# Loads and stores of a chunked product stage, in pieces of 64 KB

## The chip, the cores and the metric

The kernel runs on one core of one Trainium2 chip. The metric is the device time of one execution in microseconds (us), the median over runs. One further execution was recorded by the hardware profiler, and all views of the profile come from it.

## The reference

The input x has 16 samples of 128 x 1024 float32 values. Two blocks follow one another, each with a mixer and a feed-forward part, both added to x. The first block's feed-forward part is the one that matters here. It is a spectral filter, run along the 1024 positions of a sample, each with 128 channels:

```
Vf = rfft(phi, n); Uf_p = rfft(u, n); Uf_m = rfft(u * sign, n)
U_plus  = irfft(Vf[.., k, .] * Uf_p);  U_minus = sign * irfft(Vf[.., k, .] * Uf_m)
out = sum over k, d of (U_plus s_k M_plus[k, d, e] + U_minus s_k M_minus[k, d, e]) + short taps
```

Four such filters are mixed by weights. The mixing over 16 filters k and over the channels d and e is linear, so it can be done at each frequency: a matrix per frequency, made of the filters' spectra and the matrices M, multiplied with the spectra of all 16 samples. Attention, convolutions and a routed mixture of experts make up the rest.

## The kernel before

The kernel has three stretches. **Up to about 383 us** an attention stage and the forward transform run through the samples. For each sample, POOL writes the spectrum into a tile xf, and SP stores it into a DRAM tensor vd of shape [16 chunks, 128, 16 samples, 128 values] (line 627; for the last sample in two DMAs, chunk 0 first). SP also stores the sample's running sum x to a DRAM tensor xd (line 646), and loads mi, x and weights.

**From about 383 to 661 us** runs the product stage, the one that is changed. It loops over 16 chunks c of frequencies, and in each over four steps m.

- `begin(c)` (called with c + 1 in step m = 0 of chunk c) loads the chunk's spectra from vd, in four DMAs of four samples each into four tiles xc with one buffer per tile (line 793, 128 rows of 2 KB, 256 KB each), and POOL makes the tile v from each: two additions or subtractions (L796) and one negation (L797).
- `generate` computes, on PE, the matrices of the next chunk into PSUM tiles pg (L805; 64 matmuls as the profile counts them per step), and `collect` copies them to the tile g on DVE (L816) and ACT (L818).
- `multiply` multiplies v with g on PE into a PSUM tile py (L829; 64 per step). ACT copies py to yt (L891), and `combine` adds and subtracts the halves into a tile ys on DVE (L858, L859).
- `finish(c)`, after the last combine of a chunk, does four more operations on POOL (L843 to L846; on DVE for the last chunk) and stores ys into a DRAM tensor yd, in two DMAs of 128 rows of 4 KB (line 850, 512 KB each). The last two chunks go to a tensor of their own, yd[1].

v and ys have two buffers each, and the PSUM pool eight, shared by pg and py. In chunk 15 nothing is generated any more, so its four steps are products alone.

The order on PE, DVE, ACT and POOL is the order of the program text in this stage. The order on SP, which issues all these DMAs, is left to a planner that works from its own estimates. In its order SP issues three xc loads of chunk 0, then the last sample's two vd stores and its xd store, then nine xc loads (the fourth of chunk 0, those of chunks 1 and 2), and from there on two yd stores of chunk c and four xc loads of chunk c + 3 in turn. Behind the stores of chunk 13 stand loads for the next stretch (gw, gb, tmat, wi), then the stores of chunks 14 and 15. The DMAs that SP issues signal on eight semaphores in turn, so each also waits until the one eight before it has landed.

**From about 661 us** the inverse transform, convolutions, routing and experts run. Their first work waits for a load y from yd.

Of the kernel before, what the change touches and what calls it, by code (L numbers as in the profile page):

```python
# [14 lines left out]
P = 128  # L15
B, C, H, W = 16, 128, 32, 32
# [16 lines left out]
NCH = 16  # L33
# [7 lines left out]
RG = P // KR  # L41
# [28 lines left out]
def metaformer_kernel(ctx: ExitStack, tc: tile.TileContext, io: dict, out: bass.AP):  # L70
    nc = tc.nc
# [104 lines left out]
    with ExitStack() as l0:  # L176
# [3 lines left out]
        vd = dram.tile([NCH, P, B, CW], F32, name="vd", tag="vd")  # L180

        yd = [dram.tile([n, 2, B, 2 * NM, C], F32, name=f"yd{i}", tag=f"yd{i}")
              for i, n in enumerate((P - 2 * JL, 2 * JL))]
# [36 lines left out]
        with ExitStack() as a0:  # L220
# [537 lines left out]
            with tc.manual_schedule(engines=PINNED):  # L758
                for p in range(-reach, B):
                    next(preparing, None)  # L760
                    for name, d in period:
                        b = p + d
# [13 lines left out]
        with ExitStack() as g0:  # L776
# [8 lines left out]
            def begin(c):  # L785

                v = cpl.tile([P, 2 * NM * JL, 3, B], F32, name="v", tag="v")
                vs[c] = v
                vv = v.rearrange("p (x w) k b -> p x k b w", x=2)
                for i in range(B // BP):  # L790
                    bs = slice(i * BP, (i + 1) * BP)
                    xc = xcl.tile([P, BP, 2, 2, NM * JL], F32, name="xc", tag=f"xc{i}")
                    nc.sync.dma_start(xc.rearrange("p b x r w -> p b (x r w)"), vd[c, :, bs, :])
                    e, o = (xc[:, :, x].rearrange("p b r w -> p r b w") for x in range(2))
                    for x, op in enumerate((ALU.add, ALU.subtract)):
                        nc.gpsimd.tensor_tensor(vv[:, x, 1:, bs], e, o, op)  # L796
                    nc.gpsimd.tensor_scalar(v[:, :, 0, bs], v[:, :, 2, bs], -1.0, None, ALU.mult)  # L797
# [40 lines left out]
            def finish(c, ys):  # L838

                eng = nc.gpsimd if c + 1 < NCH else nc.vector  # L840
                e = cpl.tile([P, JL // RG, 2, C], F32, name="ye", tag="ye", bufs=1)
                yv = ys[:, :, 0]
                eng.tensor_tensor(e, yv[:, :, :2], yv[:, :, 2:], ALU.add)  # L843
                eng.tensor_tensor(yv[:, :, 2:], yv[:, :, :2], yv[:, :, 2:], ALU.subtract)
                eng.tensor_tensor(yv[:, :, 0], e[:, :, 0], e[:, :, 1], ALU.add)
                eng.tensor_tensor(yv[:, :, 1], e[:, :, 0], e[:, :, 1], ALU.subtract)  # L846
                for kl in range(JL // RG):
                    last = c + 2 >= NCH
                    j0 = kl * RG + (c - NCH + 2 if last else c) * JL
                    nc.sync.dma_start(  # L850
                        yd[last][j0 : j0 + RG].rearrange("g r b x e -> (g r b) (x e)"),
                        ys[:, kl].rearrange("p x m e -> p (x m e)"),
                    )

            def combine(c, m, ys, t):

                a, b = t
                nc.vector.tensor_tensor(ys[:, :, 0, m], b, a, ALU.add)  # L858
                nc.vector.scalar_tensor_tensor(ys[:, :, 1, m], b, -1.0, a, ALU.mult, ALU.add)  # L859
                if m == NM - 1:  # L860
                    finish(c, ys)

            with tc.manual_schedule(engines=PINNED):
                begin(0)
                gs[0] = gpl[0].tile([P, CW, C], F32, name="g", tag="g")
                for q in range(NB):
                    collect(0, q, generate(0, q))
                waiting = None
                for c in range(NCH):
                    if c + 1 < NCH:  # L870
                        gs[c + 1] = gpl[(c + 1) % 2].tile([P, CW, C], F32, name="g", tag="g")

                    ys = cpl.tile([P, JL // RG, 2, NM, C], F32, name="ys", tag="ys")
                    for m in range(NM):
                        if c + 1 < NCH:
                            pg = [generate(c + 1, 2 * m + x) for x in range(2)]
                            collect(c + 1, 2 * m, pg[0])
                        if waiting:
                            combine(*waiting)
                        if c + 1 < NCH:  # L880
                            if m == 0:
                                begin(c + 1)
                            collect(c + 1, 2 * m + 1, pg[1])
                        py = psg.tile([P, 2, JL // RG, C], F32, name="py", tag="p")
                        fresh = set()
                        for x in range(2):
                            multiply(c, m, x, py, fresh)
                        if c + 1 < NCH or m == 0:
                            t = cpl.tile([P, 2, JL // RG, C], F32, name="yt", tag="yt", bufs=1)
                        if c + 1 < NCH:  # L890
                            nc.scalar.copy(t, py)  # L891
                            waiting = c, m, ys, (t[:, 0], t[:, 1])
                        else:
                            nc.scalar.copy(t[:, m % 2], py[:, 0])
                            waiting = c, m, ys, (t[:, m % 2], py[:, 1])
# [14 lines left out]
    with ExitStack() as c1:  # L910
# [695 lines left out]
        with tc.manual_schedule(engines=PINNED):  # L1606
            yt = first.tile([P, 2, N], F32, name="yt", tag="v")
            for pr in (0, 1, 2, 3, 7, 4, 5, 6):
                py = [ps.tile([P, N], F32, name=f"pfy{j}", tag="pfy") for j in range(2)]
                for hf in range(2):  # L1610
                    cs = slice(hf * HALF, (hf + 1) * HALF)
                    for j in range(2):
                        js = slice(j * E, (j + 1) * E)
# [3 lines left out]
                for j in range(2):  # L1617
                    b = 2 * pr + j
# [162 lines left out]
```

## Time and profile before

| what | value |
|---|---|
| median of 3 runs (lowest, highest) | 1250.93 us (1250.57 to 1251.35) |
| profiled execution: time, span | 1249.26 us, 1247.5 us |
| busy, share of the span | PE 93%, PE weight load 76%, DVE 75%, ACT 58%, POOL 48% |
| product stage, 399 to 646 us (247.00 us): busy | PE 238.59, DVE 181.89, ACT 184.66, POOL 200.77 us |
| the same window: share of the DMA engines, rate | 0.39, 123 GB/s |
| loads xc<-vd | 64 DMAs of 256 KB, median 3.4 us to landing |
| stores yd<-ys | 32 DMAs of 512 KB, median 3.6 us to landing |
| DMA queue q1 (hardware, from SP) | 90448 packets, 170.46 MB |
| DMA queue q8 (instructions) | 113 packets, 1.85 MB |

The profiled execution has 1.76 us around its span, and lies 1.67 us under the median of the runs. A line such as "L829" is a line of the kernel before. PEld is the weight load that precedes a matmul and overlaps the one before it. SPq stands for SP's queue, where a row's duration is the time that the issue takes, not the transfer. In a row of groups or of the timeline, the bracket at the end gives the idle time of the engine before the work and what ended it. The granted clock of PE was 0.994 on average.

### The profile page before, as it was taken

The numbers are of one execution on the slowest core, as the hardware profiler recorded it, in microseconds if no ns is written. First come the engines' busy times: TensorE is split into PE (matmuls) and PEld (weight loads), VectorE is DVE, ScalarE is ACT, GpSimd is POOL, SyncE is SP. The second block draws the span as 40 slices with busy tenths as digits, with TensorE's granted clock in tenths as the row PEclk, the third lists the DMA queues.
The fourth block names the chain that finished last, engine by engine and source line by source line (L and its number), as shares of the span: only waits on it lengthen the run. The fifth ranks groups of instructions, "written<-read, shape, count | busy, mean of one in ns | idle before, by whom it ended". The sixth has DMA issues, their size and how long they took to land.

```text
span 1247.5 us, 34359 instructions
## 1 busy us (share of the span) xinstructions
PE 1166.0 (93%) x14398; PEld 952.3 (76%) x14398; DVE 940.9 (75%) x1944; ACT 725.2 (58%) x1420; POOL 603.1 (48%) x800
## 2 busy tenths in 40 slices
PE   7889999999999999999988899999999999998996
PEld 6667777776768898888887788888888888875443
DVE  5888888888766777777765689898898989884235
ACT  4777777877556777777751346555555556534111
POOL 2435545665568688888882434343333334220003
PEclk9999999999999999999999999999999999999998
DMA  7005344352436334444348422233332331416996
GB/s 279 24 31 168 118 135 132 117 173 90 137 119 211 105 115 138 139 129 127 128 128 277 121 51 54 84 101 118 115 106 85 102 102 51 152 43 240 384 406 279
DMA packets 91244, 175.14 MB, mean 140 GB/s; under 512 B 5969, under 2 KB 42065, under 8 KB 90449
## 3 DMA queue, kind: packets, MB, share of 16 engines
q1 hardware_dynamic: 90448, 170.46, 41.2%
q0 software_dynamic: 640, 2.49, 0.6%
q8 instruction: 113, 1.85, 0.6%
q14 instruction: 43, 0.34, 0.1%
HBM read 110.28 MB, written 62.65 MB: 139 GB/s over the span
## 4 chain that ended last, share of the span: by engine, by line
PE 60%; DVE 23%; ACT 7%; DMA 4%; issue 4%; POOL 2%; SPq 0%; POOLq 0%; ACTq 0%; DVEq 0%
PE pg L805 10%; PE pcv L988 10%; PE py L829 10%; PE big L638 6%; DVE bst L135 4%; PE big L152 3%; PE big L171 3%; PE big L570 2%; PE big L450 2%; PE big L533 2%; PE big L432 2%; DMA y<-yd 2%; DVE abss L1231 1%; DVE xp L1253 1%; ACT tt L144 1%
## 5 line engine op out<-in xcount | busy, mean ns | idle before, releaser
L988 PE MATMUL pcv<-v,cw 128*128 128x256 f32 x1152 | 259.9, 382 | 2.7 <-POOL v L1178 2.7
L988 PEld LDWEIGHTS pcv<-v,cw 128*128 128x128 f32 x1152 | 215.9, 191 | 36.3 <-issue 4.9
L818 ACT COPY g<-pg 128x512 f32<-128x512 f32 x316 | 161.1, 605 | 46.0 <-PE pg L805 45.3
L816 DVE COPY g<-pg 128x512 f32<-128x512 f32 x196 | 127.6, 682 | 69.4 <-PE pg L805 69.4
L805 PE MATMUL pg<-ph,mst 32*128 32x128 f32 x4096 | 144.2, 280 | 9.2 <-issue 8.2
L805 PEld LDWEIGHTS pg<-ph,mst 32*128 32x128 f32 x4096 | 128.7, 186 | 25.7 <-issue 16.7
L829 PE MATMUL py<-g,v 128*32 128x128 f32 x4096 | 125.1, 274 | 4.6 <-issue 2.3
L829 PEld LDWEIGHTS py<-g,v 128*32 128x32 f32 x4096 | 108.2, 110 | 12.7 <-POOL v L797 2.6
L144 ACT ACTIVATE tok<-tok,sts 128x128 f32<-128x128 f32 x256 | 101.9, 481 | 16.9 <-DVE sts L1065 13.6
L135 DVE BATCH_NORM_STATS2 bst<-big 128x6 f32<-128x256 f32 x256 | 91.1, 416 | 21.0 <-PE big L152 11.7
L796 POOL TENSOR_TENSOR v<-xc 128x256 f32<-128x256 f32 x128 | 99.0, 797 | 3.3 <-PE pg L805 2.3
L638 PE MATMUL big<-u,mu 128*128 128x128 f32 (+4 forms) x384 | 86.0, 380 | 0.0
L1178 POOL TENSOR_TENSOR v<-abss 128x256 f32<-128x256 f32 x64 | 49.1, 787 | 68.1 <-DVE abss L1174 56.7
L286 POOL TENSOR_TENSOR xf<-ab 128x256 f32<-128x256 f32 x34 | 24.8, 729 | 110.4 <-DVE ab L253 110.3
L1197 POOL TENSOR_TENSOR yo<-abss 128x256 f32<-128x256 f32 x32 | 23.5, 735 | 110.2 <-DVE abss L1193 110.2
L638 PEld LDWEIGHTS big<-u,mu 128*128 128x128 f32 x384 | 56.7, 191 | 18.0 <-issue 15.4
L570 PE MATMUL big<-wf,ub 128*128 128x256 f32 x256 | 62.0, 385 | 0.2
L144 ACT ACTIVATE tt<-tt,sts 128x128 f32<-128x128 f32 x128 | 51.1, 481 | 14.5 <-DVE sts L1065 14.5
L797 POOL TENSOR_SCALAR v<-v 128x256 f32<-128x256 f32 x64 | 55.7, 871 | 5.6
L475 POOL TENSOR_TENSOR ke<-ke,ks 128x1024 f32<-128x1024 f32 x16 | 30.6, 1914 | 54.8 <-DVE qs L483 43.8
L1622 POOL TENSOR_TENSOR xb<-yt,xb 128x1024 f32<-128x1024 f32 x3 | 7.1, 2355 | 96.9 <-ACT yt L1621 96.9
L570 PEld LDWEIGHTS big<-wf,ub 128*128 128x128 f32 x256 | 46.2, 190 | 8.8 <-ACT xn L423 3.0
(256 smaller groups left out, 2526.0 us busy)
## 6 DMA issues: line engine op xcount, KB each, us to landing
we<-in_weight SPq DMA_DIRECT2D x32, 1024.0 KB, 8.9
xc<-vd SPq DMA_DIRECT2D x64, 256.0 KB, 3.4
yd<-ys SPq DMA_DIRECT2D x32, 512.0 KB, 3.6
vd<-xf SPq DMA_DIRECT2D x15, 1024.0 KB, 5.1
y<-yd SPq DMA_DIRECT2D x15, 896.0 KB, 6.7
x<-in_x SPq DMA_DIRECT2D x16, 512.0 KB, 4.7
mi<-in_M_phi SPq DMA_DIRECT2D x16, 512.0 KB, 4.8
xd<-x SPq DMA_DIRECT2D x16, 512.0 KB, 6.1
```

What stands on the lines that cost most here:

```text
L135: nc.vector.bn_stats(bst[:, j : j + 2, :].rearrange("p j s -> p (j s)"), src[:, j : j + 2, :].rearrange("p j c -> p c j"),)
L144: nc.scalar.activation(dst[:, j, :], src[:, j, :], AF.Identity, bias=nm[:, j : j + 1], scale=r[:, j : j + 1],)
L570: nc.tensor.matmul(dst, self.ub[:, q, :], wf[:, q, :], start=True, stop=True)
L638: nc.tensor.matmul(self.pa[:, a:hi], mu[:, NF - 1 - si, tap, :], self.u[:, a - tap : hi - tap], start=(tap == 0), stop=(tap == KU - 1),)
L796: nc.gpsimd.tensor_tensor(vv[:, x, 1:, bs], e, o, op)
L797: nc.gpsimd.tensor_scalar(v[:, :, 0, bs], v[:, :, 2, bs], -1.0, None, ALU.mult)
L805: nc.tensor.matmul(pg[r][:, i], mst[rs, 4 * q + i, :], ph[rs, c, :], start=True, stop=True,)
L816: nc.vector.tensor_copy(dst, src)
L818: nc.scalar.copy(dst, src)
L829: nc.tensor.matmul(py[rows, x, kl, :], v[:, (x * NM + m) * JL + jl, 1 - ri : 3 - ri, :] .rearrange("p k b -> p (k b)"), g[:, ((x * 2 + ri) ...
L988: nc.tensor.matmul(pc[:, i], wt[:, dy, k, :], v[:, k, dy * WT : dy * WT + HT], start=(dy == 0), stop=(dy == 2),)
L1178: nc.gpsimd.tensor_tensor(v[:, k, WT : WT + HT], self.ab[:, 0], self.ab[:, 1], op)
```

## The change

In `begin`, each of the four loads of a chunk is replaced by four loads of 32 rows of 2 KB, 64 KB each. In `finish`, each of the two stores is replaced by eight stores of 16 rows of 4 KB, 64 KB each; for the last chunk both stay whole. Together that makes 256 loads for 64 and 242 stores for 32. Tiles, buffers, the work of the compute engines and its order are the same.

```
@@ begin
-  nc.sync.dma_start(xc.rearrange("p b x r w -> p b (x r w)"), vd[c, :, bs, :])
+  for js in (slice(j, j + P // 4) for j in range(0, P, P // 4)):
+      nc.sync.dma_start(
+          xc[js].rearrange("p b x r w -> p b (x r w)"), vd[c, js, bs, :]
+      )
@@ finish, in the loop over kl
-  nc.sync.dma_start(
-      yd[last][j0 : j0 + RG].rearrange("g r b x e -> (g r b) (x e)"),
-      ys[:, kl].rearrange("p x m e -> p (x m e)"),
-  )
+  dst = yd[last][j0 : j0 + RG].rearrange("g r b x e -> (g r b) (x e)")
+  n = B if c + 1 < NCH else P
+  for k in range(0, P, n):
+      nc.sync.dma_start(
+          dst[k : k + n], ys[k : k + n, kl].rearrange("p x m e -> p (x m e)")
+      )
```

The planner's order on SP for the changed program: three 64 KB pieces of the first load of chunk 0, then the last sample's two vd stores and its xd store, then 45 pieces (the fourth piece of the first load, the other twelve of chunk 0, and those of chunks 1 and 2), and from there on 16 store pieces of chunk c and 16 load pieces of chunk c + 3 in turn. POOL's first operation on a tile xc waits for four DMAs where it waited for one. DVE's first write into a ys buffer waits for sixteen where it waited for two.

## Prediction

> **What bounds the kernel now.** I began with part 1 of the page: PE is busy 93% of the span, and part 2 shows its clock granted in full. The table by stage gives PE 238.59 of 247.00 us busy from 399 to 646 us, so in the product stage PE sets the pace and the other engines follow. Next comes the timeline of PE alone (start, duration, work, idle time before it):
>
> ```profile
> 406.61 2.07 PE L805 MATMUL pg<-ph,mst 32*128 32x128 f32 x64
> 408.61 1.95 PE L829 MATMUL py<-g,v 128*32 128x128 f32 x64
> 410.50 2.07 PE L805 MATMUL pg<-ph,mst 32*128 32x128 f32 x64
> ...
> 470.16 1.95 PE L829 MATMUL py<-g,v 128*32 128x128 f32 x64
> 472.05 0.93 PE L805 MATMUL pg<-ph,mst 32*128 32x128 f32 x19
> 473.30 1.61 PE L805 MATMUL pg<-ph,mst 32*128 32x128 f32 x45 [0.32 <-issue]
> ```
>
> Undisturbed, a step of m takes (414.38 - 402.73)/3 = 3.88 us, a chunk of four 15.53. From 402.73 (chunk 0, m=2) to the products of chunk 14, m=3, at 643.93 there are 57 steps and one generation of 2.0 us: 57 x 3.88 + 2.0 = 223.2 us. It took 241.2. **18.0 us are lost**, 1.2 a chunk, some 15 to 20 matmuls into a generation, and the waits (waiting group, who was waited for, us, times, longest) name no engine:
>
> ```profile
> PEld pg L805 <- issue: 15.9, 40, 1.2
> PE pg L805 <- issue: 8.2, 16, 1.1
> ```
>
> Those two lines give only the visible gaps (0.2 us of each weight-load gap is ordinary); the rest is generations stretched to 2.2 to 2.5 us. "issue" here is PE without instructions, as the next view shows. Part 3 has a queue that carries them, and the DMA view in narrow windows shows when (queue and kind: packets, MB, share of 16 engines). First the window 468 to 470 us, just after both stores of a chunk were issued at 467.09 and 467.46:
>
> ```profile
> q1 hardware_dynamic: 212, 0.80, 98.9%
> ```
>
> and then the half microsecond from 470.5:
>
> ```profile
> q8 instruction: 1, 0.02, 12.0%
> ```
>
> While 1 MB of results drains, no instruction packet starts; one starts at 470.96, as the burst ends, and PE, dry since 472.98, resumes at 473.30. Windows around the stores at 483.59 and 500.65 read alike: packets at 487.7 and 505.0, PE resuming at 490.08 and 507.36, each about 2.4 us after the packet began. A second, smaller delay comes with the 256 KB loads (packet 509.76, PE resuming 512.18).
>
> The queue of SP is the other thing to read, at the start of the stage:
>
> ```profile
> 382.97 1.27 SPq L793 DMA_DIRECT2D xc<-vd  x3
> 384.50 0.80 SPq L627 DMA_DIRECT2D vd<-xf  x2
> 385.39 3.95 SPq L646 DMA_DIRECT2D xd<-x  x1
> 389.77 16.34 SPq L793 DMA_DIRECT2D xc<-vd  x9
> ```
>
> and in the middle, where each group of loads is spread over 7.5 us by waits for buffers, so SP is mostly idle:
>
> ```profile
> 467.09 0.80 SPq L850 DMA_DIRECT2D yd<-ys  x2
> 468.66 7.74 SPq L793 DMA_DIRECT2D xc<-vd  x4
> 483.59 0.80 SPq L850 DMA_DIRECT2D yd<-ys  x2
> ```
>
> Up to the stage's last stores, the only DMAs of the stage among the long pieces of the chain that ended last are at that start (384.50 vd<-xf 5.21 us, 389.77 xc<-vd 4.92 us); the last stores are the third (660.44, 5.13 us).
>
> [...] The 64 KB load of tmat landed in 2.1 us here, so a piece is mostly latency; that matters only where someone waits for it.
>
> **The change part by part.**
>
> *Bytes and compute* are the same, and so is the order on PE, ACT, DVE and POOL. SP's program grows by 402 DMAs: loads 64 to 256, stores 32 to 242 (the last chunk keeps 2 whole ones).
>
> *The burst goes.* [...] A fetch then finds at most a piece or two ahead. An undisturbed fetch: boundary about 0.95 us into a generation, packet about 0.6 us later (412.02 for the generation of 410.50), 0.9 to 1.3 us long, PE going on 1.4 us after its end: about 3.2 us against 3.88 between boundaries. That leaves 0.7 us, enough for a piece or two, not for every mix with loads. I take three quarters of 18.0 us: **-13.5 us** (bounds 0, if the wait has another cause, and -18.0).
>
> *SP's issue rate.* Price: durations are 0.32 us after a pause, and in a row 0.43 with 0.05 between. At the start of the program:
>
> ```profile
> 2.13 0.44 SPq L190 DMA_DIRECT2D lw<-in_gumbel  x1
> 2.62 0.91 SPq L315 DMA_DIRECT2D x<-in_x  x2
> 3.57 0.44 SPq L736 DMA_DIRECT2D wf<-in_wf  x1
> ```
>
> that is 0.475 us each. A chunk now issues 32: 15.2 us, against 15.53 us of PE. It just fits. In the chunk, with F the end of finish on POOL: stores F to F+7.6, loads of the chunk after next F+7.6 to F+15.2. POOL wants their first part at F+15.5 and it lands by about F+12; the ys buffer is written again at F+14.5 and its stores land by F+10.5. So 3.5 us of slack on both, and **0 us** at this price. Each DMA also waits for the one eight before it (eight semaphores in turn): 8 x 0.475 = 3.8 us against a landing of 2 to 3 us, no wait. Bounds: 0.37 us (0.32 + 0.05) gives nothing more; 0.55 is priced below. Extra waits on POOL (three more per load) and on DVE (8 lanes before ys is reused) are taken by the sequencers ahead of time while the engine still works (semaphore instructions of 17 to 50 ns): 0, at most 0.2 us a chunk.
>
> *The start.* In the planned SP order three pieces, not three whole loads, stand before the stores vd (two) and xd of the last sample; the fourth piece of the first load stands behind them, then the other 12 of chunk 0. Before, POOL began v of chunk 0 at 386.80 with three loads there, waited 0.94 us for the fourth and ended at 397.13; PE idled 1.20 us for it. After, POOL's first operation needs the fourth piece: it can be issued when xd's issue ends, 385.39 plus 1.2 to 3.95 us (durations of that line), I take 387.7; it lands behind 1.73 MB instead of 2.3 MB that stood ahead of the load that landed at 394.7, so 0.58 MB at some 400 GB/s, 1.4 us, sooner, and I take another 0.9 off for the earlier issue: 392.4. Then POOL's four rounds of 2.33 us (two of 0.72, one of 0.85, spacing included) follow: 401.7. The later pieces wait by their semaphores for vd and xd to land (up to 393.6) and arrive by 397, in time for round four. PE cannot go on: **+4.6 us** (bounds +3 to +7). PE sets the pace from here on, so nothing later makes it up.
>
> *The end.* PE's gap of 2.28 us at 650.94 comes with the 1 MB load of wi, still whole. Chunk 14's stores take 16 x 0.475 = 7.6 us, in part waiting for lanes behind loads of y and xp, and stand before chunk 15's two, which were issued 8.5 us after them: **+0.5 us** (0 to +2).
>
> Sum: -13.5 + 4.6 + 0.5 = -8.4 us. The profiled execution took 1249.26 us (span 1247.5, 1.76 around it): 1240.9. The median of the runs lies 1.67 us higher: **1242.5 us**.
>
> **Rivals.** *SP or its lanes become the bound (slower).* The place is SP's queue; it decides from 15.53/32 = 0.485 us a piece, 2% above my price. Later in the kernel rows of DMAs take 0.6 us each (y<-yd, 2 in 1.23 us), which speaks for it[...]. At 0.55 us a chunk needs 17.6, 2.1 more than PE: slack is gone in two chunks, then the stage runs at 17.6 instead of the present (636.22 - 417.29)/13 = 16.84 between first stores, 12 x 0.76 = +9, and +5 for start and end: about 1265. *The stalls stay*, because a fetch suffers from total traffic, not from bursts: only +5.1, 1256. Against it: the packet starts as the burst ends. *The start costs nothing*, since the piece lands early: 1238. *Halfway*: a third of the stalls gone (-6), start and end +5: 1250. [...]
>
> **How the numbers follow.** Main case 58%, 1237 to 1248; SP bound 13%; stalls stay 12%; free start 7%; halfway 10%. A measurement can tell about 0.2%, 2.5 us, from no change. Faster by more: 54 of the main case, 7 of the free start, 2 of halfway: 0.63. Within: 4, 8 of halfway, 1 of SP: 0.13. Slower: 12 + 12: 0.24. The range 1236 to 1259 takes in main case, stalls staying and the mild end of the SP case.
>
> **What would show it.** Right: a chunk near 15.9 us between first stores instead of 16.84; the two issue rows of L805 (L808 then) falling from 15.9 and 8.2 us to under half; POOL's first v<-xc near 392 and PE's first idle for POOL v at 5 us or more; SP's groups of stores about 7.6 us long. Wrong: SP without pause throughout and POOL v<-xc waiting for DMA xc<-vd in every chunk (SP bound), or issue waits as long as before (stalls stay).

## The result, and the profile after

The changed kernel takes **1291.23 us** (median, 1288.11 to 1296.54) where the kernel before took 1250.75 on the same chip: ratio 1.034, 95% interval 1.030 to 1.038. It is slower by some 40 us. I had forecast 1242.5. The lines of the code move by 3 to 6: L797, L805, L829 and L850 of before are L800, L808, L832 and L856 now, the load is L794, and POOL's first operations on xc are L799.

The profiled execution has a span of 1286.3 us against 1247.5. I split the 38.8 us at three events of the two traces: the products going on at full pace, the last product, and the first matmul of the next stage.

| stretch | before | after | difference |
|---|---|---|---|
| start of the trace to the products going on | 397.19 | 402.07 | +4.9 |
| from there to the end of the last product | 259.50 | 283.96 | +24.5 |
| from there to the first matmul big<-wi | 12.39 | 22.08 | +9.7 |
| from there to the end | 578.4 | 578.2 | -0.2 |

So it is all in the changed stage. The late start costs more than the first row says. These are the products at which PE goes on, before and after (start, duration, work, idle time before it):

```profile
397.19 1.74 PE L829 MATMUL py<-g,v 128*32 128x128 f32 x56 [1.20 <-POOL v L797]
```

```profile
402.07 3.22 PE L832 MATMUL py<-g,v 128*32 128x128 f32 x56 [0.96 <-POOL v L800]
```

After the change PE has waited 4.49 us for POOL's v, up to 400.45, and the granted clock is 0.5 from 400.4 to 407.2 us, where it was 1.0 before. So the same products take 3.22 us instead of 1.74, and by the next products, at 408.13 instead of 400.85, the stage is 7.3 us late. These other 2.4 us stand in the second row of the table.

Part 4 of the page, the chain that ended last by engine, shows the new member. First before, then after:

```profile
PE 60%; DVE 23%; ACT 7%; DMA 4%; issue 4%; POOL 2%; SPq 0%; POOLq 0%; ACTq 0%; DVEq 0%
```

```profile
PE 42%; DVE 22%; SPq 17%; ACT 6%; issue 5%; DMA 4%; POOL 3%; POOLq 0%; ACTq 0%; DVEq 0%
```

The waits between 383 and 720 us (waiting group, who was waited for, us, times, longest) say the same from the other side, over all engines and for PE's weight loads:

```profile
POOL v L799 <- DMA xc<-vd: 68.2, 16, 8.0
...
DVE ys L863 <- DMA xc<-vd: 33.7, 12, 3.5
...
PEld pg L808 <- DVE g L819: 23.4, 46, 1.9
...
PEld py L832 <- POOL v L800: 16.0, 13, 1.7
...
PEld pg L808 <- issue: 8.5, 38, 0.7
```

POOL waits for its loads once a chunk, PE then waits for POOL's v and for DVE. (What DVE waits for before it writes ys are the stores of that buffer. The row names loads, probably because loads and stores signal on the same eight semaphores.) The wait that the change was to shorten, for instructions, did shrink, from 15.9 to 8.5 us here and from 8.2 to 0.5 us in the row of the matmuls. It was replaced by something larger. The timeline of SP says what (start, duration of the issues in a row, work):

```profile
424.57 11.08 SPq L856 DMA_DIRECT2D yd<-ys  x16
435.75 9.38 SPq L794 DMA_DIRECT2D xc<-vd  x16
445.25 10.38 SPq L856 DMA_DIRECT2D yd<-ys  x16
```

From the first of these rows up to the stores of chunk 13, SP never pauses for more than 0.4 us. These groups of 16 take 9 to 11 us, not 7.6, and from the first store of chunk 0 to that of chunk 13 it is (674.51 - 424.57)/13 = 19.23 us a chunk, against 16.84 before and PE's 15.53. The pieces themselves are quick, as part 6 shows (KB each, us from issue to landing; 3.4 and 3.6 us for whole ones before):

```profile
xc<-vd SPq DMA_DIRECT2D x256, 64.0 KB, 2.1
...
yd<-ys SPq DMA_DIRECT2D x240, 64.0 KB, 2.2
```

The start and the end are in two timelines. POOL's first operation on xc comes at 392.67, where I had said 392.4:

```profile
392.67 1.43 POOL L799 TENSOR_TENSOR v<-xc 128x256 f32<-128x256 f32 x2 [8.04 <-DMA xc<-vd]
```

At the end, the last product is over at 686.03. SP has issued the last store of chunk 13 only at 682.7, and then five loads for the next stretch. The last of these, wi with 1 MB, goes out at 685.99, where before it was 646.53. Not until then come the 16 pieces of chunk 14, ahead of chunk 15's two stores, and among them SP stands still for 4.5 us: the eighth DMA after wi, at 696.03, waits until wi has landed, at 696.01. The load y that the next stage needs goes out at 704.89:

```profile
679.10 3.61 SPq L856 DMA_DIRECT2D yd<-ys  x6
...
685.99 0.43 SPq L961 DMA_DIRECT2D wi<-wid  x1
686.53 14.77 SPq L856 DMA_DIRECT2D yd<-ys  x18
704.89 0.64 SPq L1016 DMA_DIRECT2D y<-yd  x1
```

**Where SP's time goes.** Looking at single issues (the chain of waits in the narrow window 482 to 492 us; start, us, what), most cost what I had priced, 0.42 us and 0.04 to the next, but now and then one takes three to four times that:

```profile
485.60 0.42 SPq L856
486.02 0.04 issue
486.06 1.86 SPq L856
487.92 0.04 issue
487.96 0.42 SPq L856
```

The DMA view from 486.2 to 486.4 us shows what else began then (queue and kind: packets, MB, share of 16 engines):

```profile
q8 instruction: 1, 0.02, 41.3%
```

A packet of PE's instructions starts at 486.24 and takes 1.32 us, and the held issue ends 0.36 us after it. Over 13 chunks there are 54 packets and 54 issues over 0.8 us, every one beside a packet: 4.15 a chunk, 1.44 us each. So a chunk costs SP 32 x 0.464 = 14.85 us, plus 4.15 x (1.44 - 0.42) = 4.25, together 19.1 of the 19.23 measured. That was the first theory to test: **SP's issues bind, by their plain price and by being held at instruction packets.** Its rivals were the landing of small pieces, and the amount of small transfers under way.

### The profile page after: what moved, and what is told of

The parts are those of the page before. It is cut to its first block, busy times and chain, and to the rows that moved or that the text cites. A ratio compares the mean times of both kernels' runs of the same rounds, so it can differ in the third digit from the quotient of the medians.

```text
span 1286.3 us, 34907 instructions
## 1 busy us (share of the span) xinstructions
PE 1174.1 (91%) x14398; PEld 956.1 (74%) x14398; DVE 930.1 (72%) x1944; ACT 725.0 (56%) x1420; POOL 598.3 (47%) x800
## 4 chain that ended last, share of the span: by engine, by line
PE 42%; DVE 22%; SPq 17%; ACT 6%; issue 5%; DMA 4%; POOL 3%; POOLq 0%; ACTq 0%; DVEq 0%
PE pcv L993 9%; SPq L856 9%; SPq L794 8%; PE big L638 6%; DVE bst L135 4%; PE big L171 3%; PE big L152 3%; PE big L570 3%; PE big L450 2%; PE big L533 2%; PE big L432 2%; DMA y<-yd 2%; DVE abss L1236 1%; DVE xp L1258 1%; POOL v L799 1%
## 5 line engine op out<-in xcount | busy, mean ns | idle before, releaser
L808 PE MATMUL pg<-ph,mst 32*128 32x128 f32 x4096 | 146.5, 283 | 15.8 <-DVE g L819 13.2
L808 PEld LDWEIGHTS pg<-ph,mst 32*128 32x128 f32 x4096 | 130.0, 190 | 33.9 <-DVE g L819 23.4
L832 PE MATMUL py<-g,v 128*32 128x128 f32 x4096 | 131.2, 280 | 18.4 <-POOL v L800 12.3
L832 PEld LDWEIGHTS py<-g,v 128*32 128x32 f32 x4096 | 110.4, 112 | 30.2 <-POOL v L800 16.0
L799 POOL TENSOR_TENSOR v<-xc 128x256 f32<-128x256 f32 x128 | 96.8, 781 | 68.9 <-DMA xc<-vd 68.2
L896 ACT COPY yt<-py 128x512 f32<-128x512 f32 x60 | 35.2, 586 | 70.9 <-PE py L832 36.1
L800 POOL TENSOR_SCALAR v<-v 128x256 f32<-128x256 f32 x64 | 55.4, 866 | 5.6
L863 DVE TENSOR_TENSOR ys<-yt 128x256 f32<-128x256 f32 x60 | 33.1, 552 | 33.7 <-DMA xc<-vd 33.7
```

Of the source, the lines that this page charges most:

```text
L808: nc.tensor.matmul(pg[r][:, i], mst[rs, 4 * q + i, :], ph[rs, c, :], start=True, stop=True,)
L832: nc.tensor.matmul(py[rows, x, kl, :], v[:, (x * NM + m) * JL + jl, 1 - ri : 3 - ri, :] .rearrange("p k b -> p (k b)"), g[:, ((x * 2 + ri) ...
```

## The experiments

The kernels with their pieces, sorted by the time of a chunk. "Chunk" is the mean from first store to first store over 13 chunks (for the two with alternating order, from finish to finish over 14); PE's own need is 15.53 us (less in few_blocks). Half_products, sp48 and loads_only, whose chunks are not alike or not comparable, stand only in the text. Ratios are against the kernel before on the same chip.

| kernel | load, store piece (KB) | issues a chunk | chunk us | median us | ratio (95%) |
|---|---|---|---|---|---|
| mix24_ends | 64, 128, ends whole | 24 | 15.60 | 1233.57 | 0.986 (0.981 to 0.990) |
| mix24 | 64, 128 | 24 | 15.68 | 1246.74 | 0.994 (0.992 to 0.996) |
| both128 | 128, 128 | 16 | 15.92 | 1251.43 | 1.000 (0.998 to 1.003) |
| both128_ends | 128, 128, ends whole | 16 | 16.28 | 1245.41 | 0.995 (0.992 to 0.997) |
| between512 | 256, 512 in turn | 6 | 16.34 | 1250.64 | 0.998 (0.996 to 1.000) |
| loads64 | 64, 512 | 18 | 16.40 | 1254.13 | 1.000 (0.999 to 1.002) |
| stores128 | 256, 128 | 12 | 16.52 | 1250.45 | 0.997 (0.996 to 0.999) |
| few_blocks | 64, 64 | 32 | 16.64 | 1253.02 | one run |
| between64 | 256, 64 in turn | 20 | 16.70 | 1249.19 | 0.997 (0.996 to 0.999) |
| stores64 | 256, 64 | 20 | 16.83 | 1251.33 | 0.999 (0.997 to 1.002) |
| before | 256, 512 | 6 | 16.84 | 1250.75 | |
| after_end | 64, 64, last stores whole | 32 | 19.00 | 1288.35 | 1.029 (1.024 to 1.034) |
| after_start | 64, 64, first loads whole | 32 | 19.15 | 1282.52 | 1.024 (1.019 to 1.029) |
| after | 64, 64 | 32 | 19.23 | 1291.23 | 1.034 (1.030 to 1.038) |
| pinned48 | 64, 32 | 48 | 20.60 | 1309.54 | one run |

### One part of the change alone

`stores64` keeps the loads whole, `loads64` keeps the stores whole, `stores128` halves the number of store pieces:

```
stores64:  for js in (slice(0, P),):              # loads whole
loads64:   n = P                                  # stores whole
stores128: for js in (slice(0, P),):  n = 2 * B if c + 1 < NCH else P
```

> Only the stores are in pieces of 64 KB; the loads are whole, as before. Theory A (SP's queue is the bound of the changed kernel: 0.463 us per issue in a row, and about 1.0 us more whenever an instruction packet for PE is in flight while pieces are queued): 20 issues a chunk, 20 x 0.463 + some 3 x 1.0 = 12.3 us, under the 15.53 us that PE needs, so SP sets nothing. The fetch waits behind the bursts of stores go: PE from chunk 0, m=2, to the products of chunk 14, m=3, takes 223 to 229 us instead of 241.2. The start is as before (first products resumed at 397.2). Time 1233 to 1241 us. Theory B (small pieces are costly to the DMA engines or land late, whoever issues them): the stores alone bring about half of the loss of the full change, 1265 to 1275 us.

> Only the loads are in pieces of 64 KB; the stores are whole, as before. Theory A: 18 issues a chunk, 18 x 0.463 + some 3 x 1.0 = 11.3 us, so SP sets nothing. The start is delayed as in the full change: PE resumes its first products at about 402 instead of 397.2 (+4.9 us). The waits for instructions behind the bursts of stores stay, those behind whole loads go (3 to 5 us). Time 1249 to 1256 us. Theory B: half of the loss of the full change, 1265 to 1275 us.

> Stores in pieces of 128 KB, loads whole: 12 issues a chunk. Theory A with the fetch waiting behind the rate of a burst: 128 KB per 0.463 us is 283 GB/s, under the 401 GB/s at which a burst drained, so a fetch finds about one piece ahead and the stalls go as with 64 KB: 1232 to 1240 us, about the same as pieces of 64 KB. If a fetch gets through only between very small pieces, half of the gain: about 1244 us. Theory B: between before and the 64 KB stores.

`loads64` fell into its range, though its products went on at 405.0 and not at 402. None of the three is slower by a measurable amount, so neither kind of piece by itself is what costs 40 us. But stores64 and stores128 missed the range that I expected by some 10 us: with the store burst gone, PE still waits for instructions. In stores64 the store pieces keep SP busy while POOL empties its tiles, and the four loads then go out in one go (timeline of SP), after which a step of PE stalls as before (timeline of PE):

```profile
435.20 9.51 SPq L856 DMA_DIRECT2D yd<-ys  x16
444.82 2.07 SPq L794 DMA_DIRECT2D xc<-vd  x4
```

```profile
448.80 0.93 PE L808 MATMUL pg<-ph,mst 32*128 32x128 f32 x19
450.18 1.61 PE L808 MATMUL pg<-ph,mst 32*128 32x128 f32 x45 [0.45 <-issue]
```

I read this as the burst having moved from the stores to the loads. That gave a second theory: a packet is late by the amount of transfers that have piled up ahead of it.

### Half of the products

`half_products` is the changed kernel with `for ri in range(1)` in `multiply`: only the first product of each pair is computed.

> The full change, with half of the products left out (only ri = 0 is multiplied), so PE runs 768 instead of 1024 instructions a chunk and needs 3 instead of 4 instruction blocks; loads, stores and their pieces are those of the full change. Theory A: SP stays the bound, and with one blocked issue fewer a chunk takes 19.2 - 1.0 = 18.2 us between first stores. If the price of an issue or the landing of the pieces is what makes SP slow, without the instruction blocks: 19.2 us as in the full change.

It took 1341.53 us, and it doesn't price anything: the planner, with other estimates, put a chunk's store pieces ahead of the last load pieces that the next v needs, so that loads waited for finish and finish for v (POOL waited 130.9 us for xc), a chunk took 22.8 us, and PE had half its clock for some 10 of each 24 us: after 8.54 us without work a generation of 64 matmuls took 3.80 us instead of 2.07, and the granted clock was 0.938 on average. Inconclusive.

### Order, and the number of issues

`between64` and `between512` write SP's order out: after each tile that POOL has emptied come some store pieces and then the load that refills it, so that neither stores nor loads go out in one go. `mix24` and `sp48` are the changed kernel with another store piece:

```
between64: after v is made from tile i of chunk c: 4 store pieces, then the load of tile i, chunk c + 1
between512: the same with one store of 512 KB for each of the first two tiles
mix24:  n = 2 * B if c + 1 < NCH else P
sp48:   n = B // 2 if c + 1 < NCH else P
```

> Loads whole (256 KB), stores in 64 KB pieces, and the order of SP in the product stage written out: after each of the four slots that POOL empties come four store pieces and then the one load that refills that slot, instead of all store pieces and then four loads in a row; the last two chunks' stores are whole. Theory (an instruction packet of PE is late by 1 to 2 us when about 1 MB of transfers has been issued shortly ahead of it, whether two 512 KB stores or four loads pushed together): the pile is gone, late packets fall to few, a chunk takes 15.5 to 15.9 us instead of 16.85, and the time is 1234 to 1242. Rival (a packet comes late for a reason that has nothing to do with SP's transfers): a chunk stays at 16.5 to 16.9 us, 1247 to 1255. Rival (the issues of SP are held at every packet and POOL falls behind): 1255 or more, with POOL waiting for xc.

> Loads and stores whole, as before the change; only the order of SP differs: a 512 KB store, a load, the other 512 KB store, then the other three loads at POOL's pace, instead of the two stores in a row ahead of the loads. If a pile of 1 MB is needed to make a packet late, splitting it by one load and some 2 us takes part of the lateness away: chunk 15.9 to 16.5 us, 1240 to 1248. If 512 KB in one go are enough, or the transfers have nothing to do with it: 16.6 to 17.0 us and 1248 to 1256.

> Loads in 64 KB pieces, stores in 128 KB pieces: 24 issues of SP for a chunk instead of 32. Theory (SP's issues bound the changed kernel: 0.463 us each in a row, and about 1.0 us more for the one issue that is held at each of four instruction packets): 24 x 0.463 + 4 x 1.0 = 15.1 us, just below PE's 15.5, so SP has pauses again, a chunk takes 15.6 to 16.3 us, and with 5 us at the start the time is 1242 to 1252. Rival (the small load pieces or their landing cost the time, not the number of issues): a chunk stays near 18.4 us and the time at 1280 to 1292.

> Loads in 64 KB pieces, stores in 32 KB pieces: 48 issues of SP for a chunk instead of 32. Theory (SP's issues are the bound): 48 x 0.463 + 6 held issues x 1.0 = 28 us at most, 48 x 0.463 + 4 x 1.0 = 26.2 at least, some 8 us for a chunk more than with 32, 1385 to 1425. Rival (the bytes or the landing bound it): within 15 us of 1290.

`mix24` came out as the theory of SP's issues has it (1246.74 us, 15.68 us a chunk): with 24 issues SP needs 24 x 0.464 = 11.1 us at the price of after, plus 3.4 for held issues, 14.5 in all, less than PE, and then the same small load pieces cost nothing. With loads64 and stores64, which lost nothing either, landing of small pieces as the cause is out. It also holds a surprise: PE hardly stalls any more. `sp48` took 1385.92 us, inside the range, but for a wrong reason: its SP waited 57.3 us for POOL's ys, in the same loop of waits as half_products. It is no evidence on the price.

`between64` missed: 1249.19, at the rival's end. Without any pile, with single 256 KB loads between 64 KB stores, packets were late almost as often as before (15 of those between 420 and 640 us came over 4.5 us after the one ahead, against 17). That spoke against the second theory. `between512` was divided: its chunk, 16.34 us, is what the theory of the pile had forecast, its time, 1250.64 us, what the rival had. So splitting the pile takes 0.5 us off a chunk in the trace, which its total does not show.

### Both kinds in middle pieces, and the two ends

```
both128:     loads: range(0, P, P // 2);  n = 2 * B if c + 1 < NCH else P
mix24_ends:  jn = P if c == 0 else P // 4;  n = 2 * B if c + 2 < NCH else P
after_start: jn = P if c == 0 else P // 4
after_end:   n = B if c + 2 < NCH else P
```

> Loads and stores both in 128 KB pieces, 16 issues of SP for a chunk. Theory (an instruction packet of PE is late by the amount of transfers that SP has issued and that have not landed: 64 KB issued every 0.463 us is about what is moved, more than that piles up): 128 KB every 0.463 us piles up again, so some packets are late: chunk 15.9 to 16.5 us, 1240 to 1250. Rival (only a single transfer of 256 KB or more makes a packet late): chunk 15.5 to 15.7 us as with loads of 64 KB and stores of 128 KB, 1234 to 1240. In both, SP has pauses and does not bind.

> Stores in 128 KB and loads in 64 KB pieces (24 issues for a chunk), but chunk 0's loads and the last two chunks' stores whole. Theory: the middle stays at 15.7 us for a chunk, the start returns to that of the kernel before (products go on by 397 to 401 instead of 406.4) and the first matmul after the stage comes 12.5 us after the last product instead of 15.2: 5 to 10 us less than the 1246.7 of the same pieces throughout, 1236 to 1242. Rival (the late start is the stage before's, not these loads'): 1243 to 1248.

> The changed kernel with chunk 0's loads whole (4 issues instead of 16). Theory: products go on about 5 us earlier and SP, which binds from then on, has 12 issues or 5.6 us less ahead of the middle: 1284 to 1288, against 1291.2 of the changed kernel. Rival (the start costs nothing once SP binds): 1290 to 1293.

> The changed kernel with chunk 14's stores whole (2 issues instead of 16). Theory (the end is late because chunk 14's 16 issues, held at packets, stand ahead of the last stores on SP): 14 issues or some 6.5 to 9 us less at the end, the first matmul of the next stage 13 to 16 us after the last product instead of 22.1: 1282 to 1286. Rival (the end waits for the landing of the bytes, which are the same): 1290 to 1293.

`mix24_ends` is at **1233.57 us, ratio 0.986 (0.981 to 0.990)**: faster than both kernels, 1.4% below the one before, which is more than I had expected. Its products go on at 398.33 and at the full clock, and from there PE works almost at its own pace. The timeline of PE shows steps of 3.88 us without a gap, and of PE's waits between 383 and 720 us the row for instructions is down to 5.7 us (0.2 us of each gap is ordinary; its line numbers are one higher than after's):

```profile
466.21 2.07 PE L809 MATMUL pg<-ph,mst 32*128 32x128 f32 x64
468.20 1.95 PE L833 MATMUL py<-g,v 128*32 128x128 f32 x64
470.09 2.07 PE L809 MATMUL pg<-ph,mst 32*128 32x128 f32 x64
```

```profile
PEld pg L809 <- issue: 5.7, 26, 0.8
```

The gain at the end did not come: from the last product to the next stage's first matmul it is 15.6 us, in mix24 15.2; the last two stores take 7.3 and 8.1 us to land. So against mix24 nearly all of the gain is in the start.

`after_start` gained more than expected, 1282.52: the products go on at 397.79. The profiled execution of after had been mild at the start. Of the kernels with all products, the seven with split first loads go on at 402.1 (after) or at 405.0 to 406.6, and in each trace the granted clock is 0.5 there for 7 to 10 us. The nine with whole first loads go on at 397.2 to 401.0, and only both128_ends has such a stretch, of 3.4 us. `after_end` came to 1288.35, which is not clear of after's noise (its runs go from 1283.35 to 1293.57). Its trace shows an effect at the end, but less than forecast: from the last product to the next stage's first matmul it is 17.8 us instead of 22.1, where I had said 13 to 16. SP's issues explain only part of the end: chunk 15's two stores go out soon enough here, at 692.9 and 693.3, but land 9.6 and 10.5 us later (before: 3.2 and 5.1), while wi and a load that POOL issued are under way until 698.8. So the rival, that the end waits for the landing, holds for a part.

`both128` gave no gain in the total though its chunk was 15.92 us.

### What holds an issue, and where the gain of both128 went

`few_blocks` has the DMAs of the changed kernel in the changed kernel's order (written out), and fewer matmuls; `both128_ends` is both128 with whole transfers at both ends.

```
few_blocks: generate: one matmul of 512 columns for each r (was four of 128); multiply: for ri in range(1)
both128_ends: jn = P if c == 0 else P // 2;  n = 2 * B if c + 2 < NCH else P
```

> The changed kernel's DMAs, sizes and SP order in the product stage, with fewer PE instructions: a g block is generated by one matmul of 512 columns in place of four of 128 (its values are then wrong), and only the first of the two products of each pair is computed. PE has 96 matmuls for a chunk in place of 256, so some 1.5 instruction packets in place of 4. Theory (an issue of SP is held for about a microsecond at each instruction packet): 1 to 2 held issues for a chunk instead of 4, 32 issues in 15.5 to 16.6 us, a chunk 15.5 to 17 us, 1245 to 1268 in all. Rival (issues are held because of the amount of small transfers under way, packets or not): still about 4 held issues for 32, a chunk 18 to 19 us, 1283 to 1293.

> Loads and stores in 128 KB pieces, but chunk 0's loads and the last two chunks' stores whole. If the start took the gain of the 128 KB pieces (products went on at 405.5 instead of 397.2 with them): 5 to 8 us less than their 1251.4, so 1241 to 1247. Rival (the start is the stage before's and varies by itself): 1248 to 1253. In both it stays above the 1233.6 of loads in 64 KB pieces with stores in 128 KB pieces, because a chunk stays at 15.8 to 16.1 us instead of 15.6.

`few_blocks` took 1253.02 us, before beside it 1254.33. It is one execution, but the clearest of all. It asks less of PE, yet that is not what binds: SP is without a pause in both. There are 1.54 instruction packets a chunk instead of 4.15, and 1.54 held issues instead of 4.15, all 20 beside a packet. The groups of SP are about a sixth shorter for it:

```profile
446.73 7.41 SPq L793 DMA_DIRECT2D xc<-vd  x16
454.26 8.29 SPq L871 DMA_DIRECT2D yd<-ys  x16
```

32 x 0.464 + 1.54 x 1.07 = 16.5 us, against 16.64 measured. The rival, small transfers under way as such, is out: from 424 to 640 us they moved faster here (128 GB/s) than in after (112 GB/s). A packet isn't the only thing that holds an issue, though: of the 44 issues over 0.8 us in loads64, 12 have no packet beside them, each the second load piece behind two whole stores.

`both128_ends` took 1245.41, within the range: products go on at 397.95, and the start had indeed taken the gain. Its chunk, 16.28 us, was above the 15.8 to 16.1 I had expected.

### 48 issues in the changed kernel's order

```
pinned48: n = B // 2 if c + 1 < NCH else P; SP: all stores of a chunk, then all loads of the next
```

> Stores in 32 KB pieces and loads in 64 KB pieces, 48 issues for a chunk, with SP's order in the product stage the same as in the changed kernel. Theory (SP's issues are the bound): SP has no pauses. If an issue costs 0.463 us whatever its size, 48 x 0.463 + 4.2 held issues x 1.0 = 26.4 us for a chunk, 1380 to 1390; if 32 KB pieces cost the 0.345 us seen before, 32 x 0.345 + 16 x 0.463 + 4.2 = 22.6 us, 1330 to 1345. Rival (above 32 issues nothing more is lost): 1285 to 1300.

1309.54 us (before beside it 1261.23): slower than after by direction, but less than either number. SP has no pause over 0.8 us; the 32 KB issues take 0.30 us and 0.045 to the next, and only 2.0 issues a chunk are held, though there are 4.1 packets. 32 x 0.345 + 16 x 0.464 + 2.0 x 0.88 = 20.2, against 20.60 measured. So the sum holds with the prices of this trace, but neither the price nor the number of held issues carries over from 64 KB pieces. Why fewer are held is open.

### Is one whole load enough?

`loads_only` is the kernel before with a chunk's stores left to two moments:

```
rows = [c] if last else range(c, min(c + 7, NCH - 2)) if c % 7 == 0 else ()
```

> The kernel before the change, whole transfers, but the 14 stores of 512 KB of seven chunks are issued together, in chunks 0 and 7 (the rows of chunks 1 to 6 and 8 to 13 get the values of chunk 0 or 7, which are wrong), so that in chunks 3 to 6 and 10 to 13 there is nothing but four loads of 256 KB, some 2 us apart. If transfers have to pile up: no late packet in those stretches, a chunk 15.5 to 15.6 us there. If a single load of 256 KB is enough: late packets go on there, a chunk 16.0 to 16.6 us. With the stores of chunks 0 and 7 (7.3 MB in a row) packets are late in both cases. The total says little: 1240 to 1260.

This kernel leaves out the values of the other chunks' rows. The four chunks that finish between 472.5 and 538.2 us take 16.4 us each on average, the four between 592.8 and 658.3 the same. In all it took 1252.67 us (before beside it 1255.44), stores in a row included. In those chunks there is nothing but one 256 KB load every 2 us or so. One of them, in the timeline of SP, then the DMA view from 483.5 to 484.9, that from 485.0 to 485.5, and the timeline of PE:

```profile
482.35 0.32 SPq L793 DMA_DIRECT2D xc<-vd  x1
```

```profile
q1 hardware_dynamic: 119, 0.23, 55.4%
```

```profile
q8 instruction: 1, 0.02, 12.2%
```

```profile
487.56 1.61 PE L805 MATMUL pg<-ph,mst 32*128 32x128 f32 x46 [0.47 <-issue]
```

The load's data moves from 483.3 to 485.1 us; the packet starts at 485.13, 4.75 us after the one before it instead of 3.88. It is no single case. Of the 33 packets in the two stretches, 12 come more than 4.3 us after the one before, and all 12 start just as a load is ending, within 0.2 us; of the 21 others, 13 have had no load moving in the microsecond ahead. **One whole load is enough**, and the second theory is dead: a pile isn't needed. What the slow kernels have in common is the largest single transfer; that is a comparison of kernels that differ in other things too. None with a piece of 256 KB or more in the stage lost less than 0.8 us a chunk; with 128 KB of both kinds it is 0.4 and 0.75, with 128 KB stores and 64 KB loads 0.1. The loss doesn't add up over the kinds: 256 KB loads alone cost 0.9, with 512 KB stores as well 1.3, or 0.8 when the two alternate. So removing one kind buys 0.4 us a chunk at most, and nothing clear in the total. What in the queues makes a packet wait for a whole transfer was not shown.

## Why the prediction was wrong, step by step

**The stalls for instructions (-13.5 us): right in the changed kernel, with an incomplete reason.** They are gone there, but PE idles anyway for 3.7 us a chunk, which can hide a late packet. What shows that nearly all of the 18 us are to be had is mix24_ends: its chunk is 0.07 us above PE's own. But I charged them to the pair of stores and called the loads a smaller second cause. stores64, which should then have gained most of it, gained nothing; loads_only shows why. The line that I used, a packet starting just as the burst ended, was true of one burst and also, in 12 late packets of loads_only, of single loads, and the reading rested on too few packets. The "boundary" in my sum for an undisturbed fetch is the place some 0.95 us into a generation where PE ran dry at 472.98. Packets come one a step: the DMA view of before has 58 of 16.4 KB from 402.7 to 643.9 us, in 57 steps and a generation. That one packet holds the instructions of one step was my estimate from this count.

**SP's issue rate (0 us): this step failed.** The plain price was right, 0.463 us against my 0.475. What the sum lacked was a second term: 4.15 issues a chunk held for 1.02 us more at instruction packets, 4.25 us. With it the piece costs 19.1/32 = 0.60 us, beyond the decision point of 0.485 that I had named, and 3.7 us a chunk fell on a stage with 0.33 us to spare. The trace of before could not show it: there SP issues six DMAs a chunk, mostly after pauses, and none of them was held (from 399 to 646 us the longest took 0.43 us). I had priced a crowded queue from a row at the start of the program, where the DMA view has no instruction packet from 1 to 5 us. My bounds (0.37 to 0.55) were those of the plain price alone. The first rival, at 13%, named the right place, and the sign that I had given for it came: SP without a pause, and POOL waiting for its loads in every chunk. But it took a dearer plain price, 0.55 us, for what were held issues, and came to 1265. The extra waits on POOL and DVE cost no more than I had said, as far as the trace shows: POOL's line for v has 128 semaphore instructions instead of 16 and DVE's line for ys 70 instead of 28, of 43 and 50 ns in the median, and one shown, of 43 ns at 426.22 us, ran while POOL was at work from 426.21 to 427.06.

**The slack of 3.5 us held for a while.** SP started ahead, so the first chunks ran at PE's pace (15.5 us each from 408.1 to 454.7); after that every chunk paid.

**The start (+4.6 us): the mechanism was right, the size too small.** POOL and the products went on as forecast in the profiled execution, 4.9 us late, which was in part luck: in the six other kernels with all products and split first loads it was 8 to 9 us. And the sum had no term for the half clock at which PE then went on, 2.4 us in the profiled execution. after_start recovered 8.7 us in the medians.

**The end (+0.5 us): wrong, 9.7.** I counted 7.6 us for chunk 14's pieces and let most of them cost nothing, on the assumption that SP has pauses. Once SP binds, they stand behind chunk 13's and ahead of chunk 15's, and wi goes out 39 us later, so that its landing falls among the last stores.

**The landing: right.** The 64 KB pieces landed in 2.1 and 2.2 us in the median, where 256 and 512 KB had taken 3.4 and 3.6, and in the middle of the stage their landing cost nothing: loads64 is at ratio 1.000, and mix24, with the same small loads, takes 15.68 us a chunk. A piece's packets also move side by side: as a store of after begins to move, from 506.3 to 506.6 us, 11 packets of 4 KB start, which take 0.44 us each on average (DMA view: 99.8% of 16 engines), and q1 carried 6432 packets more than before, which is 16 for each of the 402 added DMAs. What cost time was the issuing, 0.60 us a piece.

## What to carry to other kernels

Before cutting DMAs into pieces, add up the issuing queue like an engine: plain price times the number, and something more for every instruction packet that falls into a row of issues; here that made 0.46 into 0.60 us. Then look for the smallest number of pieces that does the job, 24 and not 32, and keep the transfers whole that a waiting engine needs first, as at the start of this stage. At its end whole stores brought 4 us in one trace and nothing in two. When a wait is to go by making transfers smaller, all kinds of transfers in the stretch have to be cut, since here one kind that stayed whole kept most of the wait (a chunk of 16.40 us with small loads alone, 16.83 with small stores alone, 16.84 before, 15.60 with both).

## What the hardware showed that I had not expected

- With 64 KB pieces an issue in a row of DMAs is held while an instruction packet is under way: 1.44 us instead of 0.42, one for each packet (54 of 54 in after, 20 of 20 in few_blocks), ending some 0.35 us after it. With 32 KB stores it was only one for every second packet (2.0 issues and 4.1 packets a chunk in pinned48). By what mechanism an issue is held was not shown.
- The issue of a 64 KB piece takes 0.42 us in a row (median in after), that of a 32 KB piece 0.30 (pinned48), and that of a whole load after a pause 0.32 (before).
- A single 256 KB load went together with a late instruction packet, and PE was late with it: in loads_only 12 of 33 packets came more than 4.3 us after the one before, each within 0.2 us of the end of a load. The packet shown started 0.9 us late, and a chunk lost 0.9 us.
